# Turning by 64-row halves inside the half-array products of a transformer block

## The chip, the cores and the metric

The kernel runs on one core of one Trainium2 chip. The metric is the device time of one execution in microseconds: 720.22 us, the median of three runs (718.71 to 721.14). PE is TensorE, DVE is VectorE, ACT is ScalarE, POOL is GpSimd and SP is SyncE, which issues nearly all the DMAs.

## The reference

One PixArt block on x of shape (16, 256, 256): 16 batch entries, 256 tokens, width 256, 16 heads of 16, and a context of 256 tokens for each entry. Modulation vectors come from `silu(cond) @ W_mod`. Everything is float32.

```python
qkv = modulate(ln(x), shift_a, scale_a) @ W_qkv + b_qkv
x = x + gate_a * (attention(q, k, v) @ W_proj + b_proj)
q_c = ln(x) @ W_qc + b_qc
k_c, v_c = split(ln(context) @ W_kvc + b_kvc)
x = x + attention(q_c, k_c, v_c) @ W_cproj + b_cproj
h = gelu(modulate(ln(x), shift_m, scale_m) @ W_mlp1 + b_mlp1)
out = x + gate_m * (h @ W_mlp2 + b_mlp2)
```

## The kernel before

Each attention is a **unit**: 16 self-attentions (`s`) and 16 cross-attentions (`c`), 32 units n = 0 to 31 in the order s0 to s4, then s5, c0, s6, c1, ... s15, c10, and c11 to c15. A unit is computed in eight **beats** k = 0 to 7, written out by hand in `beat` (line 1103); every engine runs in program order (`InOrder`, line 39), so the order in which `beat` issues is the order on each queue. After the units comes the MLP, with whole 128-row products, which the change leaves alone.

A beat n, k holds work of several units. In `visit` (line 1079) PE first makes the scores of the *next* unit in one direction, four `s` products into the only tile `sp` (names `s<-big`), from which DVE takes the row maxima with one TENSOR_REDUCE (`s_tile`, line 697). Then come four `st` products, the scores of *this* unit the other way round with the negated maximum as an extra contraction row (row 63 of each half of `q`; `t_part`), which ACT exponentiates (`exp`, `pt<-st`). Both `sp` and `st` are single tiles: the next beat's `s` must wait for this beat's reduce, and the next `st` for this beat's exponential. In the even beats 16 `o` instructions follow (`av_part`, values times exponentials; four column strips of 32). In the odd beats 12 **slots** follow: projections of the units n+2 and n+3 and the output projection of unit n-2.

Those projections run in **lanes** (`lane`, line 451; `lanes`, line 471): a product over 128 rows is cut into two over 64, and PE's lower and upper 64 rows work on two different projections side by side, one instruction of each in a slot. A projection does its lower half in one odd beat and its upper half in the next one that has it: V and K in beat 7, Q and V in beat 1, P and Q in beat 3, K and P in beat 5. Values are float32r pairs: `xTh` and `xTl` are high and low parts. `s` and `st` also use 64-row halves (63 or 64 rows), but `o` uses all 128 rows.

Sources must be turned: a layer norm gives `xn` with tokens on partitions, and the projections want it the other way. `transposed.turn` (line 384) makes four 128x128 transpositions into one bank (`psT_s`, `psT_c`, `psT_q`), from which ACT makes `xTh`. Unit n+3's first source T[0] is turned in beats 0 and 2, two transpositions each, just after `o`. If unit n+3 is a cross-attention it has a second source T[1] (name `psT_q`), turned in beat 4. The maxima are turned as well: two per unit, one full 128-row transposition (`ident,mx`) each, in beat 0 (pairs 4 to 7 of this unit) and beat 4 (pairs 0 to 3 of the next). ACT negates them (`m`) and SP sends them into `q`. All of these are whole-array instructions that stand between `o` and the next beat's `s`.

Units n = 1 to 28 turn a T[0]; 16 of them, n = 3, 5, 7, ... 23 and 24 to 28, turn a T[1] too. Below, *with two* means a unit that turns two sources, and *with one* the 12 others.

PSUM has no room to spare: two banks for `st`, two for `sp`, one `gen` (V or P) and three `tr`, which T[0], Q, o, T[1], K, o take in turn.

Of the kernel before, what the change touches and what calls it, by code (L numbers as in the profile page):

```python
# [16 lines left out]
P = 128  # L17
# [4 lines left out]
def pixart_block(  # L22
# [53 lines left out]
    DVE.memset(wz, 0.0)  # L76
    ident = const.tile([P, P], F32, name="ident")
    make_identity(nc, ident)
    mhalf = const.tile([P, 2], F32, name="mhalf")
    POOL.memset(mhalf, -0.5)  # L80

# [295 lines left out]
    def transposed(src, name, scale=None, pool=False):  # L377

        o = Box()

        def place():
            o.ps = ps_gen(f"psT_{name}", SHORT)

        def turn(fs=range(KC)):
            if len(fs) == KC:
                place()
            for f in fs:
                for t in range(NT):
                    PE.transpose(o.ps[:, f * N + t * P:f * N + (t + 1) * P],
                                 src()[:, t, f * P:(f + 1) * P], ident)  # L390

        def high():
# [58 lines left out]
    def lane(o, half):  # L451
# [3 lines left out]
        for low in (False, True):  # L455
            for f in range(2):
                for k in range(KC):
                    for a, b in (((1, 0),) if low else ((0, 0), (0, 1))):
# [6 lines left out]
                        PE.matmul(o.ps[:, f * N:(f + 1) * N], *((x_, w_) if o.tok else (w_, x_)),  # L465
                                  start=o.fresh, stop=(half == 1 and low and k == KC - 1),
                                  skip_group_check=True)
                        o.fresh = False
                        yield

    def lanes(x, y):


        if x:
            x.ps, x.fresh = ps_gen(f"ps_{x.name}", LONG if x.tok else SHORT), True
        return zip_longest(*(lane(o, half) for half, o in enumerate((x, y)) if o))

    def run(steps, n=12):
        for _ in islice(steps, n):
# [2 lines left out]
    def to_stack(W, src, bias, dst, which, name):  # L482
# [19 lines left out]
        def high():  # L502
            o.hi = work.tile([P, KC, N], F32R, tag="qkh", name=f"h_{name}", bufs=3)
            for f in range(KC):
                ACT.activation(o.hi[:, f], o.ps[:, f * N:(f + 1) * N], AF.Identity, bias=bias[f])

        def low():
            if name == "k0":
                gap(work, 64, "gap_l")
            o.lo = work.tile([P, KC, N], F32R, tag="qkl", name=f"l_{name}", bufs=3)  # L510
            if name == "k0":
                gap(work, 192, "gap_mx")
# [66 lines left out]
    def build_pre(u):  # L579

        b = u.b
        u.mx = None
        if u.kind == "s":
            ln = layernorm(lambda: X[b], f"s{b}")
            u.ln = [ln]
# [111 lines left out]
    def s_tile(u, g, par, t, bank=None, home=sp):  # L697
# [8 lines left out]
        for j in range(2):  # L706
# [5 lines left out]
        if u.mx is None:  # L712
            u.mx = work.tile([P, 2, 2, 4, NT], F32, tag="mx", name=f"mx_{u.n}", bufs=3)
        mx = u.mx.rearrange("p f r a t -> p r f a t")
        a = slice(2 * (g % 2), 2 * (g % 2) + 2)
        if alone or apart:
            src = home[bank] if apart else sp[:, bank]
            DVE.tensor_reduce(mx[:, par, g // 2, a, t], src.rearrange("p (j n) -> p j n", j=2),
                              AX.X, ALU.max)
        elif bank == 1:  # L720
            DVE.tensor_reduce(mx[:, :, g // 2, a, t], home.rearrange("p r (j n) -> p r j n", j=2),
                              AX.X, ALU.max)
        yield

    def m_part(u, hf, pst=None):
        m_row(u, hf, m_turn(u, hf, pst))

    def m_turn(u, hf, pst=None):

        if pst is None:  # L730
            pst = ps_gen(f"psm_{u.n}_{hf}", SHORT)
        PE.transpose(pst[:16, :P], u.mx[:, hf].rearrange("p r a t -> p (r a t)"), ident)
        return pst

    def m_row(u, hf, pst):

        m = work.tile([16, P], F32R, tag="m", name=f"m_{u.n}_{hf}", bufs=1)
        ACT.mul(m, pst[:16, :P], -1.0)
        SP.dma_start(u.q[63:P:64, 4 * hf:4 * hf + 4, :].bitcast(F32), m.bitcast(F32))

    def t_part(u, pair, par):

# [22 lines left out]
    def in_turn(*pieces):  # L765

        for _ in range(2):
            for f in pieces:
                next(f)

    def av_part(u, g):

        if g % 2 == 0:
            u.po = ps_gen(f"o_{u.n}_{g}", SHORT).rearrange("p (g n) -> p g n", g=2)
        for c in range(NT):
            for h in range(4):
                par, pair = h // 2, 2 * g + h % 2
# [19 lines left out]
    for n, (kind, b) in enumerate(seq):  # L797
        u = Box()
        u.n, u.kind, u.b = n, kind, b
        u.v = vts[n % 3]  # L800
        u.q, u.k = qks[n % 3]
        u.pt = {}
        u.ready = False
        units.append(u)
    nu = len(units)

# [272 lines left out]
    def visit(n, k, home=sp, between=None):  # L1079
# [13 lines left out]
        in_turn(*t)  # L1093
        later.append(lambda: exp(units[n], k))

    def spare(n, gate=True):
        p1, _, p3 = (v and v.post for v in map(unit, (n - 1, n - 2, n - 3)))
        if p3 and not p3.added:
# [4 lines left out]
    def beat(n, k):  # L1103
# [25 lines left out]
        kp = None  # L1129
        if k == 5 and lx and n:  # L1130
            kp = lanes(q3.K, None if alone else p2)
        visit(n, k, between=kp and (lambda: run(kp, 2)))
        if k == 0:
            exps()
            if prev:
                av_part(prev, 3)
            if q3 and q3.ready:
                q3.T[0].place()
                pst = m_turn(cur, 1, q3.T[0].ps[:, N:])
                q3.T[0].turn((0,))  # L1140
            else:
                pst = m_turn(cur, 1)
            if prev:
                p1.pull_sums(1)
            m_row(cur, 1, pst)
            if q2:
                q2.K.low()
                q2.K.send_low()
# [3 lines left out]
                p2.low()  # L1152
        elif k == 1:
            exps()
            run(lanes(q2 and q2.Q, q2 and n and q2.V))
            if prev:
                p1.pull_values(1)
            if lc:
# [6 lines left out]
        elif k == 2:  # L1165
            exps()
            if cur:
                av_part(cur, 0)
            if q3:
# [8 lines left out]
        elif k == 3:  # L1178
            if q3:
                q3.T[0].high()  # L1180
            exps()
            if q3 and q3.kind == "c" and n < nu - 4:
                q3.T[0].full()
            if alone and p2:
                p2.proj(0)
                p2.proj(1)
# [1 line left out]
                run(lanes(p2, q2 and q2.Q))  # L1188
            else:
                run(lanes(q2.V, q2.Q))  # L1190
            if q3 and q3.kind == "s":
                q3.T[0].low()
            if prev and ls:
# [4 lines left out]
        elif k == 4:  # L1198
# [2 lines left out]
                p2.end()  # L1201
            if cur:
                av_part(cur, 1)
            if lx:
                lx.T[1].turn()
            if nxt:
                m_part(nxt, 0, st[:, 0] if lx else None)
            if q2:
                q2.Q.low()
                q2.Q.send_low()  # L1210
            if q3 and q3.kind == "c":
                if n < nu - 4:
                    q3.T[0].rest_pool()
                spare(n, not lc)
            if ls:
                ls.ln[0].steps[1]()
                ls.ln[0].steps[2]()
                ls.ready = True
        elif k == 5:
            exps()  # L1220
            run(kp or lanes(q3 and q3.K, (None if alone else p2) if n else q2.V))
            if cur:
                o_out(cur, 0)
            if lc:
                lc.ln[0].steps[1]()
                lc.ln[0].steps[2]()
                lc.ready = True
            if prev:
                p1.back()
            v = unit(n + 5)  # L1230
# [2 lines left out]
        elif k == 6:  # L1233
# [6 lines left out]
                cur.post.pull(0)  # L1240
            if q3 and p2:
                q3.vk = lanes(q3.V, q3.K)
                run(q3.vk, 1)
            if p3:
                p3.store()
            if lx:
                if lc:
# [3 lines left out]
        elif k == 7:  # L1251
            exps()
            if lx:
                lx.T[1].parts[2]()
            run(q3.vk if q3 and p2 else lanes(q3 and q3.V, q3 and q3.K))
            if late:
                p2.add()
                p2.added = True
# [114 lines left out]
```

## Time and profile before

| what | value |
|---|---|
| median of three runs | 720.22 us (718.71 to 721.14) |
| the profiled execution: span | 719.7 us |
| instructions in the profile | 22488 |
| mean granted TensorE clock | 0.999 |
| share of the span that DMA queue q1 took of 16 engines | 45.5% |

The profile page gives for each engine its busy time and share, the chain that ended last, and the costliest groups. The timeline lists instructions in order of time, neighbours that are alike merged into one row with a count: the first number is the start of the first in us from the start of the span, the second how long the row lasts until the end of its last one. A PE row ends only when its results are out, long after the next has started, so PE's pace is read from start to start. PEld rows are the weight loads that go ahead of the products.

### The profile page before, as it was taken

To read this page: it belongs to the slowest core of one execution; us is meant where nothing else is said; L and a number is where in the kernel's file an instruction comes from. 1 tells how busy PE (TensorE), PEld (TensorE's weight loads), DVE (VectorE), ACT (ScalarE), POOL (GpSimd) and SP (SyncE) were. 2 spreads that over 40 slices of the span, in tenths; PEclk is the share of its full clock that TensorE was granted. 3 is DMA by queue.
4 is the path that set the end of the run, shared out by engine and by line. 5 is a ranking of instruction groups with operands and counts; after the bars stand their busy time and mean duration, and the time that the engine had idled before them with its cause. 6 is when DMAs were issued, how large, how long until landed. Compare 5 with 4: busy or idle time off the path is not lost.

```text
span 719.7 us, 22488 instructions
## 1 busy us (share of the span) xinstructions
PE 710.4 (99%) x8993; PEld 592.3 (82%) x8993; DVE 567.8 (79%) x895; ACT 551.7 (77%) x955; POOL 520.6 (72%) x518
## 2 busy tenths in 40 slices
PE   9999999999999999999999999999999999999997
PEld 8777777777877778777787777777779999999997
DVE  5878888888888798888888888888675777777653
ACT  5677888888888788887888888887867677666661
POOL 7655778787776867776686798977857988656651
PEclk9999999999999999999999999999999999999999
DMA  7574455554545456454655656456323132313212
GB/s 236 183 233 157 160 170 178 175 179 160 167 151 196 162 176 191 163 166 153 195 167 176 210 174 195 156 192 196 95 78 103 59 87 61 88 46 88 66 39 74
DMA packets 81548, 106.15 MB, mean 147 GB/s; under 512 B 16610, under 2 KB 44548, under 8 KB 81444
## 3 DMA queue, kind: packets, MB, share of 16 engines
q1 hardware_dynamic: 80548, 104.37, 45.5%
q8 instruction: 71, 1.16, 0.7%
q10 hardware_dynamic: 896, 0.35, 0.2%
q14 instruction: 33, 0.27, 0.1%
HBM read 35.89 MB, written 8.98 MB: 62 GB/s over the span
## 4 chain that ended last, share of the span: by engine, by line
PE 94%; DVE 3%; POOL 2%; issue 0%; ACT 0%; POOLq 0%; ACTq 0%
PE s L51 18%; PE o L51 16%; PE st L51 16%; PE ph L51 12%; PE ps_qc L51 4%; PE ps_kc L51 4%; PE ps_k L51 4%; PE ps_q L51 3%; PE ps_v_c L51 3%; PE ps_v_s L51 3%; PE ps_P_s L51 2%; DVE mx L51 2%; PE ps_P_c L51 2%; PE psT_c L51 2%; PE psT_s L51 2%; PE psT_q L51 1%
## 5 line engine op out<-in xcount | busy, mean ns | idle before, releaser
L51 DVE TENSOR_REDUCE mx<-s 128x4 f32<-128x1024 f32 x252 | 307.9, 1222 | 73.5 <-PE s L51 70.1
L51 ACT ACTIVATE pt<-st 128x1024 f32<-128x1024 f32 x256 | 263.4, 1029 | 51.8 <-PE st L51 51.0
L51 PE MATMUL o<-pt,v 128*32 128x256 f32 x2048 | 137.1, 385 | 0.0
L51 PE MATMUL s<-big 63*128 63x256 f32 x1008 | 116.8, 305 | 1.7 <-DVE st_q L51 0.8
L51 PE MATMUL st<-big 64*128 64x256 f32 (+1 forms) x1040 | 107.7, 282 | 0.8 <-issue 0.4
L51 PE MATMUL ph<-xTh_m,wself 128*128 128x256 f32 x512 | 100.2, 281 | 0.0
L51 POOL TENSOR_TENSOR hl<-hf,hh 128x512 fp32r<-128x512 f32 x60 | 80.1, 1350 | 20.8 <-ACT hh L51 20.8
L51 PEld LDWEIGHTS s<-big 63*128 63x128 f32 x1008 | 77.3, 185 | 21.0 <-issue 7.1
L51 PEld LDWEIGHTS o<-pt,v 128*32 128x32 f32 x2048 | 53.4, 109 | 39.5 <-ACT oT L51 1.3
L51 PEld LDWEIGHTS st<-big 64*128 64x128 f32 (+1 forms) x1040 | 81.2, 186 | 3.6 <-ACT pt L51 1.5
L51 PEld LDWEIGHTS ph<-xTh_m,wself 128*128 128x128 f32 x512 | 82.3, 188 | 1.2 <-issue 0.4
L51 PE MATMUL ph<-xTl_m,wself 128*128 128x256 f32 x256 | 71.1, 278 | 0.0
L51 ACT ACTIVATE hf<-ph,bT 128x256 f32<-128x256 f32 x112 | 47.0, 473 | 22.1 <-PE ph L51 21.9
L51 ACT ACTIVATE hh<-ph,bT 128x256 fp32r<-128x256 f32 x112 | 47.0, 472 | 19.8 <-PE st L51 8.4
L51 PEld LDWEIGHTS ph<-xTl_m,wself 128*128 128x128 f32 x256 | 48.2, 188 | 0.0
L51 PE MATMUL s<-big,hh 128*128 128x256 f32 x256 | 45.6, 278 | 0.0
L51 DVE TENSOR_SCALAR xn_m<-x,mv_m,rs_m 128x256 f32<-128x256 f32 x28 | 33.5, 1237 | 14.8 <-POOL rs_m L51 14.8
L51 POOL TENSOR_SCALAR xn_q<-x,mv_q,rs_q 128x256 f32<-128x256 f32 x32 | 38.9, 1225 | 1.7
L51 POOL TENSOR_SCALAR xn_c<-c,mv_c,rs_c 128x256 f32<-128x256 f32 x32 | 38.9, 1226 | 1.7
L51 PE MATMUL st<-big,hh 128*128 128x256 f32 x224 | 40.0, 278 | 0.0
L51 PEld LDWEIGHTS s<-big,hh 128*128 128x128 f32 x256 | 38.8, 188 | 0.0
L51 POOL TENSOR_SCALAR rs_c<-mv_c 128x2 f32<-128x2 f32 x16 | 3.6, 228 | 48.3 <-DVE mv_c L51 48.2
(230 smaller groups left out, 2133.1 us busy)
## 6 DMA issues: line engine op xcount, KB each, us to landing
big<-h_k SPq DMA_DIRECT2D x32, 256.0 KB
big<-h_kc SPq DMA_DIRECT2D x32, 256.0 KB
big<-h_qc SPq DMA_DIRECT2D x32, 256.0 KB
big<-h_q SPq DMA_DIRECT2D x30, 256.0 KB
big<-l_k SPq DMA_DIRECT2D x16, 256.0 KB
g<-gd SPq DMA_DIRECT2D x16, 256.0 KB
U_s<-oT SPq DMA_DIRECT2D x32, 128.0 KB
R_s<-rd_s SPq DMA_DIRECT2D x16, 256.0 KB
```

Of the source, the lines that this page charges most:

```text
L51: i = f(*a, **k)
```

## The change

- `half(h)` turns a source by 64 rows: eight transpositions of 64x128 to 128x64 instead of four of 128x128. The lower four are made before `visit` in beat 1 (T[0]) and beat 5 (T[1]), the upper four inside the next beat's `visit`, between `s` and `st`. `turning` writes four of them and two instructions of the projection in the *other* half: t, product, t, t, product, t. The slots of beats 1 and 5 fall from 12 to 10; `uneven` runs what is left. Where there is no T[1], two plain slots are moved ahead of `visit` in beat 5.
- The maxima live in four fixed tiles `mxs` and are regrouped: pairs 2 to 5 of a unit are turned at the end of the unit before, pairs 6 and 7 together with pairs 0 and 1 of the next unit. Each group is turned by two halves (`m_half`) of 64 rows and 80 columns, in beats 2 and 3 and in beats 6 and 7, into the unused part of the bank of `o`.
- A product in the upper half waits for a copy by ACT that shows the lower half's bank is done (`behind`).
- The layer norm of a coming self-attention (aggregate on DVE, power and application on POOL) is issued in beat 5 instead of 4; the second copy of T[0] (`full`) goes ahead of the exponential of beat 3; `store` goes from beat 6 to 7.

```diff
+        def half(h):
+            rows = slice(64 * h, 64 * h + 64)
+            for f in range(KC):
+                for t in range(NT):
+                    c = f * N + t * P + 64 * h
+                    PE.transpose(o.ps[:, c:c + 64], src()[rows, t, f * P:(f + 1) * P], ident[rows, rows])
+                    yield
...
+    def turning(T, h, beside):
+        t = T.half(h)
+        for f in (t, beside, t, t, beside, t):
+            next(f)
...
+    def m_half(w, pst, h):
+        rows = slice(64 * h, 64 * h + 64)
+        PE.transpose(pst[:w.shape[1], rows], w[rows], ident[rows, rows])
...
+        if k == 1 and T0:
+            T0.place()
+            begin_of(q2.Q)
+            q2.V.behind = q2.K.copied
+            held["QV"] = side_by_side(q2.Q, q2.V)
+            turning(T0, 0, held["QV"][1])
+        if k == 5 and q3 and p2:
+            if T1:
+                T1.place()
+            begin_of(q3.K)
+            p2.behind = q2.Q.copied
+            held["KP"] = side_by_side(q3.K, p2)
+            if T1:
+                turning(T1, 0, held["KP"][1])
+            else:
+                uneven(held["KP"], 2, 2)
+        def between():
+            if k == 2 and T0:
+                turning(T0, 1, held["QV"][0])
+            if k == 6 and T1:
+                turning(T1, 1, held["KP"][0])
+            if k in (2, 6) and parts:
+                begin_o(cur, 0 if k == 2 else 2)
+                m_half(w, cur.po[:, 1, :P], 1)
+        visit(n, k, between=between)
...
-                pst = m_turn(cur, 1, q3.T[0].ps[:, N:])
-                q3.T[0].turn((0,))
...
-                q3.T[0].turn((1,) if q3.ready else (0, 1))
+            if q3 and not T0:
+                q3.T[0].turn()
...
+            m_half(w, cur.po[:, 1, :P], 0)
...
-            if lx:
-                lx.T[1].turn()
-            if nxt:
-                m_part(nxt, 0, st[:, 0] if lx else None)
```

What stands on PE around the start of beat 1, in the unit n = 17 (this unit turns `psT_c` and `psT_q`). Before, from the last `o` of beat 0:

```order
L51 MATMUL o_2_3831<-pt_7_3856,v_82 32x256
L51 MATMUL psT_c_3911<-ident,mx_3588 16x128
L51 MATMUL psT_c_3911<-ident,xn_c_3813 128x128 x2
L51 MATMUL s<-big_77 128x256 x4
L51 MATMUL st<-big_80 128x256 x4
L51 MATMUL ps_q_3939<-xTh_s_3703,wself 128x256
```

And now, at the same place:

```order
L51 MATMUL o_2_3895<-pt_7_3927,v_84 32x256
L51 MATMUL psT_c_3995<-ident,xn_c_3883 128x64
L51 MATMUL ps_v_s_3915<-wself,xTh_s_3773 128x256
L51 MATMUL psT_c_3995<-ident,xn_c_3883 128x64 x2
L51 MATMUL ps_v_s_3915<-wself,xTh_s_3773 128x256
L51 MATMUL psT_c_3995<-ident,xn_c_3883 128x64
L51 MATMUL s<-big_79 128x256 x4
```

The whole-array transpositions of the maxima and of half the source are gone from here; four half ones stand with two products of V. The second half comes in beat 2. Before, that beat ran `s`, `st` and `o`, and the transpositions followed its last `o`:

```order
L51 MATMUL o_0_3986<-pt_0_3900,v_83 32x256
L51 MATMUL o_0_3986<-pt_1_3937,v_83 32x256
L51 MATMUL psT_c_3911<-ident,xn_c_3813 128x128 x2
L51 MATMUL s<-big_77 128x256 x4
L51 MATMUL st<-big_80 128x256 x4
L51 MATMUL ps_P_s_4016<-wself,xTh_as_3924 128x256
```

Now they stand between `s` and `st`, with two products of Q and the upper half of a group of maxima, which goes into the bank of `o`:

```order
L51 MATMUL s<-big_79 128x256 x4
L51 MATMUL psT_c_3995<-ident,xn_c_3883 128x64
L51 MATMUL ps_q_3996<-xTl_s_3774,wself 128x256
L51 MATMUL psT_c_3995<-ident,xn_c_3883 128x64 x2
L51 MATMUL ps_q_3996<-xTl_s_3774,wself 128x256
L51 MATMUL psT_c_3995<-ident,xn_c_3883 128x64
L51 MATMUL o_0_4056<-ident,mxs 80x64
L51 MATMUL st<-big_82 128x256 x4
```

So after `o` nothing of the whole array is left before the next `s`, and `st` of beat 2 now stands behind a turning.

More of the change, by code (lines that the diff above doesn't have):

```diff
@@ L78, in pixart_block @@
     make_identity(nc, ident)
+    mxs = const.tile([P, 4, 80], F32, name="mxs")
+    POOL.memset(mxs, 0.0)
+    mxs = [mxs[:, i] for i in range(4)]
     mhalf = const.tile([P, 2], F32, name="mhalf")
@@ L511, in low @@
             if name == "k0":
-                gap(work, 192, "gap_mx")
+                gap(work, 192 + 128, "gap_mx")
             for f in range(KC):
@@ new lines, in m_part, with m_row @@
+    def m_part(u, hf):
+        pst = ps_gen(f"psm_{u.n}_{hf}", SHORT)[:16, :P]
+        PE.transpose(pst, mxs[2 + hf][:, :16], ident)
+        m_row(pst, (u, 4 * hf, 4))
+    def m_half(w, pst, h):
+        rows = slice(64 * h, 64 * h + 64)
+        PE.transpose(pst[:w.shape[1], rows], w[rows], ident[rows, rows])
+    def m_row(pst, *parts):
+        m = work.tile([16, P], F32R, tag="m", name="m", bufs=1)
+        ACT.mul(m[:pst.shape[0]], pst, -1.0)
+        row = 0
+        for u, pair, n in parts:
+            SP.dma_start(u.q[63:P:64, pair:pair + n, :].bitcast(F32), m[row:row + 4 * n].bitcast(F32))
+            row += 4 * n
@@ L1154, in beat @@
             exps()
-            run(lanes(q2 and q2.Q, q2 and n and q2.V))
+            if T0:
+                uneven(held["QV"], 10)
+            else:
+                run(lanes(q2 and q2.Q, q2 and n and q2.V))
             if prev:
@@ L1214, in beat @@
                 spare(n, not lc)
[L1215 to L1218, printed above, removed]
         elif k == 5:
             exps()
-            run(kp or lanes(q3 and q3.K, (None if alone else p2) if n else q2.V))
+            if q3 and p2:
+                uneven(held["KP"], 10 if T1 else 12)
+            else:
+                run(lanes(q3 and q3.K, (None if alone else p2) if n else q2.V))
             if cur:
                 o_out(cur, 0)
[L1224 to L1227, printed above, removed]
+            for l_ in (lc, ls):
+                if l_:
+                    l_.ln[0].steps[1]()
+                    l_.ln[0].steps[2]()
+                    l_.ready = True
             if prev:
@@ L1242, in beat @@
                 q3.vk = lanes(q3.V, q3.K)
-                run(q3.vk, 1)
-            if p3:
+                run(q3.vk, 0 if T1 else 1)
+            if p3 and not nxt:
                 p3.store()
```

94 lines of the change are left out of this document (56 added, 38 removed).

## The prediction

> **What bounds the kernel now.** I read the page first, then PE's timeline over one unit, then DVE's beside it.
>
> ```profile
> PE 710.4 (99%) x8993; PEld 592.3 (82%) x8993; DVE 567.8 (79%) x895; ACT 551.7 (77%) x955; POOL 520.6 (72%) x518
> ...
> PE 94%; DVE 3%; POOL 2%; issue 0%; ACT 0%; POOLq 0%; ACTq 0%
> ```
>
> PE is on 94% of the chain that ended last, so time taken off PE's queue should come off the total, as long as no other engine is just behind it. The windows of a unit with one source turned (n = 16) and one with two (n = 17), from one first `s` to the next, show who is:
>
> ```profile
> 283.54:298.83 15.29, 15.29 (x234) 11.96 (x231) 13.57 (x21) 12.70 (x21) 10.23 (x10) 1.00 0.60 190
> 298.83:314.74 15.91, 15.91 (x239) 12.45 (x237) 13.26 (x22) 13.38 (x22) 12.57 (x14) 1.00 0.45 152
> ```
>
> The columns are length, PE, weight loads, DVE, ACT, POOL, clock and DMA. PE has no gap; DVE is busy for 13.57 of 15.29 us. On averages that leaves 1.7 us a unit, but beats are less even. PE's timeline of beats 0, end of 2, 3 and 4 of n = 17:
>
> ```profile
> 298.83 0.50 PE L51 MATMUL s<-big 63*128 63x256 f32 x4
> 299.17 0.40 PE L51 MATMUL st<-big 64*128 64x256 f32 x4
> 299.50 1.07 PE L51 MATMUL o<-pt,v 128*32 128x256 f32 x16
> 300.50 0.28 PE L51 MATMUL psT_c<-ident,mx 128*16 128x128 f32 x1
> 300.62 0.38 PE L51 MATMUL psT_c<-ident,xn_c 128*128 128x128 f32 x2
> 300.93 0.51 PE L51 MATMUL s<-big 63*128 63x256 f32 x4
> ...
> 304.53 0.44 PE L51 MATMUL psT_c<-ident,xn_c 128*128 128x128 f32 x2
> 304.90 0.50 PE L51 MATMUL s<-big 63*128 63x256 f32 x4
> 305.24 0.41 PE L51 MATMUL st<-big 64*128 64x256 f32 x4
> 305.48 0.28 PE L51 MATMUL ps_P_s<-wself,xTh_as 64*128 64x256 f32 x1
> ...
> 306.85 0.42 PE L51 MATMUL s<-big 63*128 63x256 f32 x4
> 307.09 0.41 PE L51 MATMUL st<-big 64*128 64x256 f32 x4
> 307.43 1.07 PE L51 MATMUL o<-pt,v 128*32 128x256 f32 x16
> 308.43 0.66 PE L51 MATMUL psT_q<-ident,xn_q 128*128 128x128 f32 x4
> 308.95 0.28 PE L51 MATMUL st<-ident,mx 128*16 128x128 f32 x1
> 309.16 0.51 PE L51 MATMUL s<-big 63*128 63x256 f32 x4
> ```
>
> From start to start: four `s` take 0.24 after slots (306.85 to 307.09) and 0.34 after whole-array work (304.90 to 305.24), so coming back to row halves costs 0.10. Four `st` take 0.24 (305.24 to 305.48). Twelve slots take 1.37 (305.48 to 306.85), 0.114 each. `s`, `st` and `o` together take 1.60 (1.58 from 306.85, 1.67 from 298.83).
>
> **What is removed.** After `o`, the maxima and two transpositions of beat 0 take 0.43 (300.50 to 300.93), two of beat 2 take 0.37 (304.53 to 304.90), four and the maxima of beat 4 take 0.73 (308.43 to 309.16). In a unit with one source beat 4 has the maxima alone, 0.21:
>
> ```profile
> 293.06 0.28 PE L51 MATMUL psm<-ident,mx 128*16 128x128 f32 x1
> 293.27 0.50 PE L51 MATMUL s<-big 63*128 63x256 f32 x4
> ```
>
> So 1.53 us go from a unit with two and 1.01 from one with one. The return to row halves stays: something in halves still follows each `o`.
>
> **What a turning costs.** No row shows a transposition in half the rows beside a product, so I bound it. A whole one among 128-row products of the MLP:
>
> ```profile
> 548.60 0.28 PE L51 MATMUL s<-big,hl 128*128 128x256 f32 x1
> 548.72 0.60 PE L51 MATMUL psT_m<-ident,xn_m 128*128 128x128 f32 x4
> 549.08 0.36 PE L51 MATMUL ph<-xTh_m,wself 128*128 128x256 f32 x1
> ```
>
> The row of four lasts 0.60, a single one 0.28 (the maxima above): 0.32 for three steps, 0.11 each, and no pause between transposition and product. A transposition streams 128 columns; a half one streams 64, by proportion 0.055. Its weight load is still 128 columns wide, and loads show up in PEld (two answers for beat 4, one ending after the first load, one after the second; then lane products):
>
> ```profile
> 308.43 0.14 PEld L51 LDWEIGHTS psT_q<-ident,xn_q 128*128 128x128 f32 x1 [0.41 <-issue]
> 308.43 0.20 PEld L51 LDWEIGHTS psT_q<-ident,xn_q 128*128 128x128 f32 x2 [0.41 <-issue]
> ...
> 309.39 0.18 PEld L51 LDWEIGHTS ps_kc<-xTh_c,wkch 64*128 64x128 f32 x1
> 309.39 0.18 PEld L51 LDWEIGHTS ps_P_s<-wself,xTh_as 64*128 64x128 f32 x1
> 309.50 0.19 PEld L51 LDWEIGHTS ps_kc<-xTh_c,wkcl 64*128 64x128 f32 x1
> ```
>
> A second transposing load starts 0.06 after the first (0.20 less 0.14); loads of lane products follow at 0.11, the pace of the slots. I take 0.06, as the row of the same operation: four half transpositions in one half of the rows take 0.24, while the other half runs two products in 0.23. A turning is then 0.24. At least it costs 0.23, the two slots it replaces; at 0.11 a load it is 0.44. The Trainium skill speaks for the high end: "TensorE: Matmul & The Clock Gate", Part 2, section LDWEIGHTS, has a load take its columns over 1.2 per ns whatever its rows, 107 ns here, an estimate of 0.43 for a turning. The 0.06 step disagrees for transposing loads, the 0.11 of the lanes agrees; no run here shows one in half the rows. Half maxima: two pairs of halves a unit, 0.05 each (80 columns, 64 streamed), between nothing (beside the other half) and 0.12 (the whole one, 300.50 to 300.62).
>
> **The beats anew.** With two sources: beat 0 1.60 + 0.10 + 0.24 = 1.94; beat 1 0.24 + 0.24 + 10 slots = 1.62; beat 2 1.60 + 0.24 + 0.05 = 1.89; beat 3 0.34 + 0.05 + 0.24 + 1.37 = 2.00; beats 4 to 7 again 1.94, 1.62, 1.89, 2.00. Sum 14.90. With one: beat 4 1.60 + 0.10 + 0.23 = 1.93, beat 6 1.60 + 0.05 + 0.10 + 0.11 = 1.86, beat 7 0.24 + 0.05 + 0.24 + 1.25 = 1.78; sum 14.64. The same pieces in the old order give 2.03, 1.95, 1.97, 1.95, 2.33, 1.95, 1.81, 1.73 = 15.72 and, with beat 4 1.81, 15.20 (measured 15.91 and 15.29), so I compare ledger with ledger: PE alone would save 0.82 and 0.56.
>
> **What is late next.** Beats 1 and 5 get shorter than DVE's loop.
>
> ```profile
> 290.07 1.23 DVE L51 TENSOR_REDUCE mx<-s 128x4 f32<-128x1024 f32 x1 [0.56 <-PE s L51]
> 291.21 0.86 DVE L51 SCALAR_TENSOR_TENSOR xTl_s<-psT_s,sc,xTh_s 128x256 fp32r<-128x256 f32 x2
> 292.00 1.21 DVE L51 TENSOR_REDUCE mx<-s 128x4 f32<-128x1024 f32 x1
> 293.13 0.86 DVE L51 SCALAR_TENSOR_TENSOR l_qc<-ps_qc,bP,h_qc 128x256 fp32r<-128x256 f32 x2
> 293.91 1.21 DVE L51 TENSOR_REDUCE mx<-s 128x4 f32<-128x1024 f32 x1
> ...
> 307.31 1.23 DVE L51 TENSOR_REDUCE mx<-s 128x4 f32<-128x1024 f32 x1 [0.39 <-PE s L51]
> ```
>
> A reduce starts 0.46 after its `s` (306.85 to 307.31); the next `s` follows 1.27 after the reduce's start where it has waited (292.00 to 293.27); with a low part between, reduces are 1.92 apart. So `s` to `s` is at least 0.46 + 1.27 = 1.73, over the 1.62 of beats 1 and 5. The low parts of K (beat 0) and Q (beat 4) just fit: reduce 0 at 0.46, the next at 2.38 at the earliest, and `s` at 1.94 asks for it at 2.40. So beats 1 and 5 stand at 1.73, 0.11 more each. With one source T[0]'s low part follows reduce 3 and just fits as well: reduce 3 at 6.10 lets the next start at 8.02, and `s` of beat 4 at 7.56 asks for it at 8.02. Units become 15.12 and 14.86: 0.60 and 0.34 saved. Sum: 16 x 0.60 + 12 x 0.34 = 13.7 us.
>
> **The rest, at nothing.** The layer norm issued a beat later:
>
> ```profile
> 311.07 2.43 POOL L51 TENSOR_SCALAR xn_s<-x,mv_s,rs_s 128x256 f32<-128x256 f32 x2
> ```
>
> It ends at 313.50; a beat later that is 315.4, and its transposition now comes after `o` of the next beat 0, 314.74 + 1.60 = 316.3. If it is later still, PE waits with `s` and everything else queued. The new waits on ACT (`behind`) are for copies issued at the head of the same beat, 1.6 us before; were they late, the turning and `s` behind it would wait. The second copy of T[0], now ahead of the exponential of beat 3, delays it by one copy at most (0.58, the row of the same shape below), and twelve slots stand before the next `st` needs it. The upper maxima of beat 6 stand ahead of `st` and need the bank that ACT's copy of `o` frees; queued behind them are `st` and `o`, and the exponential waits for that `st`:
>
> ```profile
> 311.10 0.58 ACT L51 COPY oT<-o 128x512 f32<-128x512 f32 x1
> ```
>
> It ended 2.52 after the `s` of beat 5 (309.16). The maxima now come 1.73 + 0.48 = 2.21 after it, and `st` of beat 5, which sets ACT's start, about 0.33 sooner than in that beat (0.10 of return and 0.23 of slots that stood before it). So it just fits; half a copy late would be 0.3 x 16 = 5 us. SP gets 31 more small sends of maxima (95 for 64); those of beat 7 are needed in beat 2, over 3.5 us on. I take none of these, and no more than 5 us together.
>
> **The rivals.** First, PE's full gain, if DVE is looser than these rows: 16 x 0.82 + 12 x 0.56 = 19.8 us, 700. For it: beats 1 and 5 miss only by 0.11. Against: the 1.73 is made of rows without slack. Second, and slower: a half transposition loads at the pace of a lane product, 0.11, and a turning takes 0.44. The ledger with 0.44 gives 15.92 and 15.26, 0.20 and 0.06 more than the old one: 16 x 0.20 + 12 x 0.06 = 3.9 us slower, 724. Its place is the four (or two) turnings; each 0.1 us costs 16 x 0.4 + 12 x 0.2 = 8.8 us, so it decides from a turning of 0.24 + 13.7/88 = 0.40. The Trainium skill's rule for loads, above, comes out at the same 724. Third, the array empties between a transposition and a product of the other half, as it does around `o`: four changes of 0.10 and no overlap (0.24 + 0.23), 0.87 a turning, about 760. Against: the MLP rows change over without a pause, though there in the whole array. That the change does not do what it says can be excluded: the order shows the halves in place.
>
> **The numbers.** The sum is made against the profiled span, 719.7, which lies 0.5 under the median 720.22 and inside its 718.71 to 721.14; I take 13.7 off the median: 706. Its own range is 699 to 714 (half a copy of `o` or 0.06 a turning up, half the DVE term down). Chances: forecast 0.62; first rival 0.08; a turning between 0.30 and 0.38 (711 to 718) 0.07, of which 0.05 faster; second rival 0.14, of which 0.08 inside 722; third 0.06; others slower 0.03. What can be told from no change is 0.3%, 2.2 us. Faster: 0.62 + 0.08 + 0.05 = 0.75; same 0.10 (the rest of the third case and the second where it lands under 722); slower 0.15. The range 698 to 722 leaves out the slow cases and the ends, under 0.2.
>
> **What would show it.** Right: `psT` rows of 64 columns 0.06 apart beside slots at 0.11; units of about 15.1 to 15.3 and 14.9 to 15.0 us; `s` of beats 2 and 6 waiting for DVE by about 0.1; no wait at the upper maxima of beat 6. Wrong: half transpositions 0.11 or more apart, products of the other half standing still meanwhile, PE waiting for ACT's copy of `o` or POOL's `xn`, or units still at 15.3 and 15.9.

## The result and the profile after

The changed kernel takes 716.07 us (median of 5 runs, 714.10 to 717.74), the kernel before 719.89 us (5 runs, 718.71 to 721.14, on the same chip): a ratio of 0.9948 with a 95% interval of 0.9928 to 0.9967. It is faster by 3.8 us, where 13.7 us were forecast. The profiled execution spans 715.5 us in place of 719.7. The page of the kernel after, its engines and its chain:

```profile
PE 705.1 (99%) x9233; PEld 593.9 (83%) x9233; DVE 564.5 (79%) x895; ACT 551.0 (77%) x956; POOL 520.6 (73%) x519
...
PE 93%; DVE 3%; DMA 1%; issue 1%; POOL 1%; ACT 0%; SPq 0%; POOLq 0%; ACTq 0%
```

PE has 240 instructions more and is busy 5.3 us less; 1% of the chain is now DMA, which was not on it before. The windows of the same two units (n = 16 with one source, n = 17 with two) in the kernel after:

```profile
280.95:296.25 15.30, 15.30 (x241) 12.16 (x239) 13.57 (x21) 12.55 (x21) 10.34 (x10) 1.00 0.58 187
296.25:311.84 15.59, 15.59 (x250) 12.40 (x247) 13.18 (x22) 13.46 (x22) 12.44 (x13) 1.00 0.43 147
```

They were 15.29 and 15.91. By these, a unit with two sources gains 0.32 of the 0.60 that were forecast, one with one source nothing of its 0.34. The beats say where. This table has the median time from the first `s` of a beat to the first `s` of the next, over units 1 to 28, read from PE's timeline; the last rows belong to experiments below.

| kernel | sources | beat 0 | 1 | 2 | 3 | 4 | 5 | 6 | 7 | sum |
|---|---|---|---|---|---|---|---|---|---|---|
| before | two | 2.06 | 2.00 | 1.97 | 1.95 | 2.31 | 1.97 | 1.83 | 1.79 | 15.89 |
| forecast | two | 1.94 | 1.73 | 1.89 | 2.00 | 1.94 | 1.73 | 1.89 | 2.00 | 15.12 |
| after | two | 1.96 | 1.92 | 1.94 | 1.97 | 1.95 | 1.92 | 1.94 | 1.97 | 15.57 |
| before | one | 2.05 | 2.00 | 1.95 | 1.95 | 1.79 | 1.96 | 1.84 | 1.80 | 15.34 |
| forecast | one | 1.94 | 1.73 | 1.89 | 2.00 | 1.93 | 1.73 | 1.86 | 1.78 | 14.86 |
| after | one | 1.95 | 1.92 | 1.93 | 1.97 | 2.00 | 1.74 | 2.00 | 1.76 | 15.27 |
| e2, turning behind st | two | 1.84 | 2.04 | 1.92 | 1.98 | 1.83 | 2.05 | 1.95 | 1.96 | 15.57 |
| e3, other bank | two | 1.84 | 2.04 | 1.93 | 1.96 | 1.83 | 2.05 | 1.95 | 1.96 | 15.56 |
| e9, slot ahead | two | 1.91 | 1.85 | 2.02 | 1.97 | 1.90 | 1.85 | 2.07 | 1.96 | 15.53 |
| e15, no low parts | two | 1.96 | 1.81 | 2.03 | 2.00 | 1.95 | 1.80 | 2.05 | 2.00 | 15.60 |
| e5, short reductions | two | 1.95 | 1.69 | 1.92 | 1.98 | 1.95 | 1.69 | 2.16 | 2.00 | 15.34 |
| e5, short reductions | one | 1.94 | 1.69 | 1.93 | 2.00 | 1.99 | 1.63 | 1.90 | 1.80 | 14.88 |
| e6, before, short reductions | two | 2.00 | 1.95 | 1.95 | 1.95 | 2.31 | 1.96 | 1.83 | 1.80 | 15.76 |
| e6, before, short reductions | one | 2.02 | 1.95 | 1.94 | 1.95 | 1.79 | 1.95 | 1.83 | 1.75 | 15.17 |
| e7, and no half maxima | two | 1.87 | 1.69 | 1.87 | 1.97 | 1.89 | 1.69 | 1.87 | 1.97 | 14.81 |
| e7, and no half maxima | one | 1.88 | 1.70 | 1.90 | 1.95 | 1.92 | 1.63 | 1.86 | 1.85 | 14.69 |

All beats with two sources but 1 and 5 are within 0.05 of the forecast. Beats 1, and 5 with two, stand at 1.92 and not at 1.73; beat 5 with one does stand at 1.74, but beat 6 behind it at 2.00 and not at 1.86. PE's weight loads at the end of beat 0 and in beat 1 of n = 17 show the turning and what comes behind it:

```profile
297.92 0.13 PEld L51 LDWEIGHTS psT_c<-ident,xn_c 64*128 64x128 f32 x1 [0.41 <-issue]
297.93 0.18 PEld L51 LDWEIGHTS ps_v_s<-wself,xTh_s 64*128 64x128 f32 x1
297.98 0.14 PEld L51 LDWEIGHTS psT_c<-ident,xn_c 64*128 64x128 f32 x1
298.04 0.19 PEld L51 LDWEIGHTS ps_v_s<-wself,xTh_s 64*128 64x128 f32 x1
298.04 0.20 PEld L51 LDWEIGHTS psT_c<-ident,xn_c 64*128 64x128 f32 x2
...
298.39 0.31 PEld L51 LDWEIGHTS st<-big 64*128 64x128 f32 x4
298.86 0.18 PEld L51 LDWEIGHTS ps_q<-xTh_s,wself 64*128 64x128 f32 x1 [0.16 <-DVE l_k L51]
```

Half transpositions load 0.06 apart (297.92, 297.98, 298.04) while the other half's products go on at 0.11 (297.93, 298.04): the turning takes about 0.24. But the first product of Q waits for DVE's `l_k`. Q takes over the bank of K, and the low part of K is what reads that bank last. DVE in the same beats:

```profile
296.80 1.22 DVE L51 TENSOR_REDUCE mxs<-s 128x4 f32<-128x1024 f32 x1
297.94 0.87 DVE L51 SCALAR_TENSOR_TENSOR l_k<-ps_k,bqkv,h_k 128x256 fp32r<-128x256 f32 x2
298.73 1.22 DVE L51 TENSOR_REDUCE mxs<-s 128x4 f32<-128x1024 f32 x1
...
300.57 1.23 DVE L51 TENSOR_REDUCE mxs<-s 128x4 f32<-128x1024 f32 x1 [0.48 <-PE s L51]
```

The low part ends at 298.81 and Q starts at 298.86. So the first theory (A) was that this wait costs beats 1 and 5 their 0.19; its rival (B), that the turning itself, or coming back from it, does. The experiments found a third answer.

There are also single stalls. Units 1 to 28 took 440.28 us before and 438.76 after. By the medians, 16 x 0.32 + 12 x 0.07 = 6.0 us went; 4.5 us came back in a few units, most of all n = 23 (2.5 us over its kind) and 24 (1.3). PE's waits, SP's queue and windows of the kernel after at that place:

```profile
PE s L51 <- DMA big<-l_q: 2.2, 1, 2.2
```

```profile
397.30 1.20 SPq L51 DMA_DIRECT2D big<-m  x2
398.55 0.39 SPq L51 DMA_DIRECT2D cb<-cd  x1
398.98 0.43 SPq L51 DMA_DIRECT2D w<-in_L_xcond_W_mlp_dram  x1
399.45 1.23 SPq L51 DMA_DIRECT2D big<-h_q  x2
400.78 0.58 SPq L51 DMA_DIRECT2D big<-l_q  x1
```

```profile
403.00:407.30 4.30, 2.10 (x33) 1.91 (x34) 2.09 (x3) 2.55 (x6) 1.64 (x3) 1.00 0.94 238
407.30:411.50 4.20, 4.18 (x42) 2.77 (x44) 2.36 (x4) 1.61 (x2) 3.07 (x3) 0.59 0.69 234
```

The loads of the MLP's bias and first weight (`cb`, `w`) go out in front of Q's high and low parts. The DMA engines are 94% busy from 403.0 to 407.3, PE stands 2.2 us for `l_q` and then runs at a granted clock of 0.59. SP's queue at the same place in the kernel before:

```profile
399.24 0.32 SPq L51 DMA_DIRECT2D rd_c<-S_c  x1
399.62 0.42 SPq L51 DMA_DIRECT2D cb<-cd  x1
400.09 0.42 SPq L51 DMA_DIRECT2D w<-in_L_xcond_W_mlp_dram  x1
402.36 1.18 SPq L51 DMA_DIRECT2D big<-h_q  x2
```

There the loads went out 2.3 us and more ahead of Q's parts, 6.4 us into the unit; now it is 9.3 us. In between stand the two sends of maxima (`big<-m`) that the change puts at the end of beat 3: SP sends in order, and they go out at 397.30, when ACT's `m` is ready (397.27). Over the whole execution SP waits 58.9 us for `m`, where it waited 15.7.

### The profile page after: what moved, and what is told of

Same layout as the page of the kernel before. It is cut to its first block, busy times and chain, and to the rows that moved or that the text cites. A ratio compares the mean times of both kernels' runs of the same rounds, so it can differ in the third digit from the quotient of the medians.

```text
span 715.5 us, 23043 instructions
## 1 busy us (share of the span) xinstructions
PE 705.1 (99%) x9233; PEld 593.9 (83%) x9233; DVE 564.5 (79%) x895; ACT 551.0 (77%) x956; POOL 520.6 (73%) x519
## 4 chain that ended last, share of the span: by engine, by line
PE 93%; DVE 3%; DMA 1%; issue 1%; POOL 1%; ACT 0%; SPq 0%; POOLq 0%; ACTq 0%
PE s L51 18%; PE o L51 17%; PE st L51 16%; PE ph L51 12%; PE ps_qc L51 4%; PE ps_kc L51 4%; PE ps_q L51 4%; PE ps_k L51 3%; PE ps_P_s L51 3%; PE ps_v_s L51 2%; PE ps_v_c L51 2%; PE ps_P_c L51 2%; DVE mxs L51 2%; PE psT_m L51 1%; PE psT_s L51 1%; DMA big<-l_q 1%
## 5 line engine op out<-in xcount | busy, mean ns | idle before, releaser
L51 DVE TENSOR_REDUCE mxs<-s 128x4 f32<-128x1024 f32 x252 | 308.0, 1222 | 73.1 <-PE s L51 70.7
L51 PE MATMUL s<-big 63*128 63x256 f32 x1008 | 121.0, 302 | 3.6 <-DMA big<-l_q 2.2
L51 PE MATMUL st<-big 64*128 64x256 f32 (+1 forms) x1040 | 119.4, 288 | 0.4 <-ACT pt L51 0.4
L51 PEld LDWEIGHTS s<-big 63*128 63x128 f32 x1008 | 83.2, 186 | 31.4 <-DVE mxs L51 22.9
L51 PEld LDWEIGHTS st<-big 64*128 64x128 f32 (+1 forms) x1040 | 91.2, 186 | 3.0 <-ACT pt L51 1.5
L51 PE MATMUL ps_P_s<-wself,xTh_as 64*128 64x256 f32 x256 | 42.0, 294 | 0.0
L51 PE MATMUL ps_v_s<-wself,xTh_s 64*128 64x256 f32 x224 | 39.7, 299 | 0.0
```

Of the source, the lines that this page charges most:

```text
L51: i = f(*a, **k)
```

## The experiments

Ratios are to the kernel before, run on the same chip.

**e1, the bank freed by ACT.** `low()` of Q and K reads the high part instead of the bank:

```diff
-DVE.scalar_tensor_tensor(o.lo[:, f], o.ps[:, f * N:(f + 1) * N], bias[f], o.hi[:, f], ...
+DVE.scalar_tensor_tensor(o.lo[:, f], o.hi[:, f].bitcast(F32), bias[f], o.hi[:, f], ...
```

> The changed kernel, but in the units of the steady state the low parts of Q and K are worked out from the high parts in SBUF instead of from the PSUM bank (so the low parts of these are wrong, and the output with them); DVE still runs an instruction of the same shape at the same place. The bank that the next lane products need is then freed by ACT's copy alone. Theory A (the first slot of Q in beat 1, and of K in beat 5 with two sources, waits for DVE's low part, which frees its bank): beats 1, and 5 with two, fall from 1.92 to 1.73-1.76 us, 44 beats x 0.17 = 7.5 us: about 0.984 of the kernel before, 708 us (706 to 711). Rival B (the half transpositions, or the coming back to row halves, cost PE that time): beats 1 and 5 stay at 1.92, 716 us (0.995).

759.22 us, 1.0557 (1.0530 to 1.0584). A miss of both, because the instruction put in was not the same in cost. DVE and POOL in beats 0 and 1 of one unit of this run:

```profile
323.00 2.20 DVE L51 SCALAR_TENSOR_TENSOR l_k<-h_k,bqkv 128x256 fp32r<-128x256 f32 x2
```

```profile
322.88 0.61 POOL L51 CAST xTh_as<-U_s 128x512 fp32r<-128x512 f32 x1
323.57 1.35 POOL L51 TENSOR_TENSOR xTl_as<-U_s,xTh_as 128x512 fp32r<-128x512 f32 x1
```

With both operands in SBUF the low part takes 2.20 us in place of 0.87, and ends (325.20) when POOL's work does (324.92). The next reduction is late, and beat 1 takes 2.85 us. One thing can be read: Q's first product now comes 0.55 after `s` (median) in place of 0.67, so the wait for the bank is 0.12 long.

**e2, turning behind `st`.** The first half turning goes to where PE waits for the bank. The order of the two halves then has to be kept by something else than `s`: a one-column ACT copy of the turned half, for which the second half waits. The line that goes stood ahead of `visit`, the new one stands behind it and `exps`; T[1] alike in beat 5.

```diff
-            turning(T0, 0, held["QV"][1])
...
+                turning(T0, 0, held["QV"][1])
...
+        if h == 0:
+            T.seen = ACT.activation(dummy[:, :1], T.ps[:, 384:385], AF.Identity)
```

> The changed kernel, with the first half turning of each source moved from ahead of the s of beats 1 and 5 to behind their st (one tiny ACT copy per source is added, to order the two halves). Theory A: the turning fills part of the wait for the bank. s of beat 1 goes at 1.73 (DVE's loop), Q's first slot at 2.55 after the s of beat 0 (reduce 0.46 + 1.21, low part 0.86), ten slots and the return: 3.72 for beats 0 and 1 in place of 3.87; 44 x 0.15 = 6.6 us: 709.5 us (708 to 712), 0.986. Rival B: the turning costs the same wherever it stands: 716 us, 0.995.

714.79 us, 0.9939 (0.9921 to 0.9957). Beats 0 and 1 are 1.84 and 2.04, 3.88 together in place of 3.88: PE no longer waits for the bank, but now `s` of beat 1 waits for DVE's reduction.

**e3, another bank.** K is given its bank ahead of T[1] (with one source an empty tile takes T[1]'s turn), so Q takes over T[1]'s bank; the first half turning stands behind the fourth slot.

```diff
+            begin_of(q3.K)
             if T1:
                 T1.place()
-            begin_of(q3.K)
+            else:
+                ps_gen(f"none_{n}", SHORT)
...
+                uneven(held["QV"], 4, 4)
+                turning(T0, 0, held["QV"][1])
+                uneven(held["QV"], 6, 6)
```

> The changed kernel, with K given its bank ahead of T[1] (with one source, an empty place in the ring of three takes T[1]'s turn), so that Q takes over a bank that POOL or ACT freed long before and K one that was freed in beat 3 or 4; the first half turning moves behind the fourth slot of beats 1 and 5 (with the same tiny ACT copy). Theory A: no wait is left in beats 1 and 5; beats 0 and 1 together are held by DVE's loop alone, 0.46 + 1.92 + 1.27 = 3.65 in place of 3.87: 44 x 0.22 = 9.7 us, 706.5 us (705 to 710), 0.981. Rival B: 716 us, 0.995.

716.22 us, 0.9948 (0.9931 to 0.9965). The wait for `l_k` is gone from the waits of PE's weight loads, and beats 0 and 1 are 1.84 and 2.04 again; the loads of `s` now wait for DVE's reduction 102 times in place of 53. Theory A falls: the wait for the bank is there, but taking it away gives nothing back.

**e4, the loads behind Q.** The first entry of `W1P` goes from (-9, 3) to (-9, 4).

> The changed kernel, with the load of the MLP's bias and first weight issued one beat later (after beat 4 of unit 23 instead of after beat 3), so that they stand behind the sends of Q's high and low parts on SP. Theory A (PE's 2.2 us wait at the end of unit 23, and the slow clock behind it, come from l_q queued behind these loads): 716 - 3.7 = 712.5 us, 0.990. Rival (a delay of that one execution): 716 us, 0.995, and the wait at the same place or nowhere.

714.68 us, 0.9939 (0.9918 to 0.9960). Unit 23 takes its normal 15.55, but unit 24 takes 2.0 us over its kind: DVE stands for the context, whose load is now the one behind the weights, and with it the reduction of beat 2. DVE's waits for DMA in this run:

```profile
DVE st_c L51 <- DMA c<-in_ctx_dram: 1.7, 1, 1.7
```

**e5 and e6, DVE out of the way.** In both kernels the reductions of `s` take half of the columns.

```diff
-            DVE.tensor_reduce(..., home.rearrange("p r (j n) -> p r j n", j=2),
+            DVE.tensor_reduce(..., home.rearrange("p r (j n) -> p r j n", j=2)[:, :, :, :N // 2],
```

> The changed kernel with every reduction of s taken over half of its columns (the maxima are those of half of the keys, so the output isn't the reference's): DVE's loop falls from 1.73-1.82 to about 1.2 us, and the low parts end 0.6 us earlier, so that neither DVE nor the bank holds PE. What is left is PE's own work. Theory C (PE's pieces are larger than the prediction's ledger, and the waits of beats 1 and 5 are only a part): beats 1.95, 1.74, 1.94, 1.97 twice, units of 15.2 and 15.0 us; 716 - (16 x 0.37 + 12 x 0.29) = 706.6 us, 0.981 (0.978 to 0.985). Rival P (the ledger of PE was right, 14.90 and 14.64, and waiting for DVE took the rest): 716 - 18.4 = 697.6 us, 0.969.

> The kernel before with the same half reductions: what PE alone takes in the old order. Theory C: the old order waits for DVE little, units 15.7 and 15.2 in place of 15.89 and 15.34: 720 - 4.4 = 715.6 us, 0.994, so that PE alone gains about 9 us by the change. Rival P: the same here, but then PE alone gains 18 us.

After: 709.19 us, 0.9842 (0.9803 to 0.9881). Before: 714.69 us, 0.9925 (0.9900 to 0.9950). Between them are 5.5 us, where theory C had 9; units 23 and 24 of the changed kernel are 3.5 us over their kind in this run too. Two units of the changed kernel with short reductions (n = 16, 17):

```profile
278.62:293.50 14.88, 14.88 (x241) 12.00 (x239) 9.68 (x21) 12.50 (x21) 10.38 (x10) 1.00 0.57 189
293.50:308.87 15.37, 15.37 (x250) 12.36 (x248) 9.02 (x21) 13.47 (x22) 12.45 (x13) 1.00 0.47 159
```

DVE is busy for 9.0 and 9.7 us of a unit, and units still take 15.37 and 14.88. Beats 1 and 5 do fall to 1.69. Rival P (697.6) is out; theory C comes close (706.6), but beat 6 with two sources rises to 2.16. PE there, and ACT beside it:

```profile
305.11 0.28 PE L51 MATMUL psT_q<-ident,xn_q 64*128 64x64 f32 x2
305.39 0.25 PE L51 MATMUL o<-ident,mxs 64*80 64x64 f32 x1
305.39 0.54 PE L51 MATMUL st<-big 64*128 64x256 f32 x4
```

```profile
304.76 0.58 ACT L51 COPY oT<-o 128x512 f32<-128x512 f32 x1
```

The upper half of the maxima waits until ACT's copy of `o` (to 305.34) has freed the bank, and `st` behind it too: the wait that the prediction named and took at nothing. In the changed kernel itself it isn't there (1.94), because DVE holds PE back first. Without it, 0.24, PE's own unit is 15.10 with two sources.

**e7, no half maxima**, in the run with short reductions:

```diff
-                m_half(w, cur.po[:, 1, :P], 1)
...
-            m_half(w, cur.po[:, 1, :P], 0)
...
-        m_row(cur.po[rows_, 1, :P], *parts)
+        m_row(ident[rows_], *parts)
```

> The run with the changed kernel and half reductions, without the half transpositions of the maxima (ACT writes the row of maxima from a constant, so no maximum is subtracted before the exponential; all else stands). By the prediction's 0.05 for each, four to a unit: 30 x 0.20 = 6 us less than with them. Theory C (each puts the two row halves out of step, and the next whole-array work waits for the later half): 0.08 to 0.10 each, 10 to 12 us less. If they lie beside other work: no difference.

700.75 us, 0.9755 (0.9709 to 0.9802): 8.4 us less than with them. With one source the four halves cost 0.19 (forecast 0.20), with two 0.53, of which 0.24 is the wait in beat 6 and 0.29 their own. They show in beats 0 and 4 (1.95 to 1.87 and 1.89), one beat later than they run: the half that turned is behind the other, and `o`, which takes the whole array, waits for the later one.

**e8, the maxima alone.** `T0 = T1 = None`; the sources are turned whole, as before.

> The changed kernel with the sources turned whole at the places of the kernel before (two transpositions behind o in beats 0 and 2, four in beat 4), so that of the change only the maxima in halves and groups and the later layer norms are left. By the prediction's pieces: two whole maxima go (0.09 and, in beat 4, 0.18 or 0.11), four halves at 0.05 come: 0.07 less a unit, 718 us (0.997). Theory C with 0.09 a half: 0.09 more a unit, 722.5 us (1.003).

737.42 us, 1.0243 (1.0221 to 1.0266). With two sources the run is spoilt (K takes Q's bank right behind Q's low part, and beat 4 takes 2.96). With one source it can be read: 15.67 against 15.34 before, 0.33 more where theory C had 0.09 and the prediction's pieces 0.07 less. So with whole sources the half maxima are a loss. The run does not show how much of it is theirs alone: the later layer norms and, with one source, the two slots ahead of `s` in beat 5 are still there.

**e9, one slot ahead.** e3, with one slot of Q and V (or K and P) ahead of the `s` that waited:

```diff
+            uneven(held["QV"], 1, 1)
...
-                uneven(held["QV"], 4, 4)
+                uneven(held["QV"], 3, 3)
```

> The run with the other bank, with one slot of the lane pair moved ahead of the s of beat 1 (and of beat 5 with two sources), so that PE has work where it waited there for DVE's reduction, and comes to s already in row halves. Theory C (freeing the bank alone moved the wait to that s, 0.16, and made the s behind it a slow one): beat 0 is 1.67 + 0.22 = 1.89 and beat 1 0.24 + 0.24 + 0.24 + 9 x 0.114 + 0.09 = 1.84, 3.73 for the pair, and DVE allows 3.74 (reduce 1 at 2.46 with the low part between, 1.23, 0.05): 3.74 to 3.80 in place of 3.87, 44 x 0.10 = 4.4 us, 711.5 us (709 to 714), 0.988. Theory D (DVE's reduce, low part, reduce hold the pair at 3.86 in any order): 716 us, 0.995.

715.38 us, 0.9955 (0.9939 to 0.9972). The pair is 1.91 + 1.85 = 3.76, as theory C had it, and yet nothing is gained: beat 2 rises from 1.94 to 2.02. Its `s` has now waited for DVE.

**e10 and e11, whole maxima behind `o`**, one transposition each in beats 2 and 6, in the changed kernel and in e9.

> The changed kernel with the grouped maxima turned whole behind o of beats 2 and 6 in place of four halves. In the run with short reductions the four halves cost 0.31 with two sources and 0.19 with one; two whole ones cost 0.12 each by the row of before: 0.07 less with two, 0.05 more with one. Theory C: beats 0 and 4 fall by 0.07 (the halves come to o in step), beats 2 and 6 rise by 0.07: 716 us (714 to 717), 0.995. By the prediction's 0.05 a half: 0.04 more a unit, 717.2 us, 0.996.

> The run with the slot ahead and the whole maxima together: the sum of the two by theory C, 710.5 us (708 to 714), 0.987.

719.82 us, 1.0017 (1.0000 to 1.0033), and 721.48 us, 1.0046 (1.0032 to 1.0060): both misses. In e10 beats 0 and 4 fall by 0.06 to 0.10 as expected, but beats 2 and 6 rise by 0.13 to 0.20: the whole one starts 1.00 after the first `o`, where the next `s` starts in the changed kernel, and the next `s` comes 0.24 later, not 0.12.

**e12, e13 and e14, the loads early.** The first four entries of `W1P` go from beat 3 to beat 1, in e11, in the changed kernel and in e9.

> The run with both, and the MLP's bias and first four weight loads issued two beats earlier (after beat 1 of units 23 to 26, where the DMA engines are idle, instead of after beat 3, ahead of the sends of Q's high and low parts). Theory A (PE's wait for l_q at the end of unit 23, 2.2 us, and the half clock behind it, 1.3 us, are theirs): 3 us less than without, 707.5 us (705 to 711), 0.983, and no wait of over 0.7 us in units 23 and 24. Rival (another transfer is late in their place): no difference.

> The changed kernel, with nothing changed but the MLP's bias and first four weight loads, issued two beats earlier (after beat 1 of units 23 to 26). Theory A (the waits of units 23 and 24 are these loads' doing, in the changed kernel as well): about 2.7 us less than the changed kernel, as between the two runs with both: 713.4 us (712 to 715), 0.991, no wait over 0.7 us in units 23 and 24. Rival: 716 us, 0.995.

> The run with the slot ahead, with the same early loads: 715.4 - 2.7 = 712.7 us (711 to 715), 0.990.

718.83 us, 1.0005 (0.9992 to 1.0018); 713.36 us, 0.9903 (0.9880 to 0.9925); 712.67 us, 0.9895 (0.9873 to 0.9918). That is 2.65, 2.71 and 2.71 us less than the same kernel without; only the first pair ran on the same chip, and by the ratios the other two are 0.0045 and 0.0060 apart. (In the profiled e11 most of the stall, 1.7 us, stood in unit 26, where the last of the four loads goes out.) SP's queue in e13, unit 23:

```profile
394.07 0.59 SPq L51 DMA_DIRECT2D cb<-cd  x1
394.70 0.45 SPq L51 DMA_DIRECT2D w<-in_L_xcond_W_mlp_dram  x1
...
398.87 1.22 SPq L51 DMA_DIRECT2D big<-h_q  x2
400.19 0.54 SPq L51 DMA_DIRECT2D big<-l_q  x1
```

The loads go out 4 us ahead of Q's parts, in a pause of the queue and ahead of the maxima's sends, and no beat of units 23 and 24 stalls. e14 is the fastest version that ran, ahead of both kernels.

**e15, no low parts.** DVE's low parts of Q and K are left out; the reductions stay.

```diff
+            if name not in ("k0", "k1", "q0", "q1"):
+                o.lo = o.hi
+                return
```

> The changed kernel without the low parts of Q and K in the units of the steady state (the high part is sent in their place, so all three products use it; the sends stay): DVE has 0.87 us less in beats 0 and 4, and ACT's copy alone frees the bank. Theory C (the low parts hold beats 1 and 5, as they stand between two reductions and free the bank): beats 1, and 5 with two, fall from 1.92 to 1.73-1.77, units of 15.25 to 15.35 and 15.1 us: 716 - 6 = 710 us (708 to 712), 0.987. Rival D (the reductions alone, 1.83 from one waiting s to the next, hold the beats): 716 us, 0.995.

716.00 us, 0.9944 (0.9923 to 0.9965): rival D. DVE and PE in beats 1 and 2 of n = 17 of this run:

```profile
299.07 1.23 DVE L51 TENSOR_REDUCE mxs<-s 128x4 f32<-128x1024 f32 x1 [0.70 <-PE s L51]
300.21 0.24 DVE L51 BATCH_NORM_AGGREGATE mv_q<-st_q 128x2 f32<-128x6 f32 x2
300.89 1.23 DVE L51 TENSOR_REDUCE mxs<-s 128x4 f32<-128x1024 f32 x1 [0.45 <-PE s L51]
```

```profile
298.54 0.48 PE L51 MATMUL s<-big 63*128 63x256 f32 x4
...
300.35 0.51 PE L51 MATMUL s<-big 63*128 63x256 f32 x4
300.69 0.28 PE L51 MATMUL psT_c<-ident,xn_c 64*128 64x64 f32 x2
```

The same `s` of beat 2 and what follows it, in the changed kernel:

```profile
300.12 0.42 PE L51 MATMUL s<-big 63*128 63x256 f32 x4
300.38 0.28 PE L51 MATMUL psT_c<-ident,xn_c 64*128 64x64 f32 x2
```

DVE is idle for 0.70 ahead of the reduction, no low part is near and no bank is waited for. The reduction starts 0.53 after `s` (298.54 to 299.07), ends at 300.30, and the next `s` starts at 300.35: 1.81. And behind an `s` that has waited, the next work starts 0.34 later (300.35 to 300.69); behind one that came straight after slots, 0.26 (300.12 to 300.38; the median is 0.24). So the beat costs 1.81 and 0.10 more in the one behind it: 1.91, against 1.92 with the wait for the bank. Two limits of DVE, one through the bank and one through the reduction, stand at the same height, and whichever is lifted leaves the other.

## Why the prediction was wrong, and what was right in it

**Right.** PE bounds the kernel, and the change is faster, though 716.07 lies outside the sum's own 699 to 714. The turning by halves costs what was taken, 0.24, in spite of the weight loads: 0.06 apart beside products (the second rival, 724 us, had 0.11). The Trainium skill's rule ("TensorE: Matmul & The Clock Gate", Part 2, section LDWEIGHTS: a load takes its columns over 1.2, an estimate of 107 ns here) is not borne out by the 0.06 between the first and the second `psT_c` load above. The third rival, an array that empties between the halves (760), is out by the same rows. So is the first, PE's full gain (700), by beats 1 and 5. The layer norm a beat later costs one wait for `xn_s`, 0.6 us in unit 1, which e13 shows too (0.3) and e2, e3 and e4 don't; the `behind` waits cost nothing that PE's rows show.

**The step that failed** is "The beats anew" together with "What is late next". That DVE's loop becomes the bound in beats 1 and 5 was right, and was the mechanism; its size was not. "So `s` to `s` is at least 0.46 + 1.27 = 1.73" used a reduction that starts 0.46 after its `s`, as it does behind slots. Behind a turning it starts 0.53 after `s`, and an `s` that has waited gives 0.10 more to the beat behind it. 1.73 becomes 1.91, and beats 1, and 5 with two, came out at 1.92. With one source beat 5 is 1.74, as worked out, and the 0.10 is found in beat 6 (2.00 in place of 1.86). "The low parts of K (beat 0) and Q (beat 4) just fit" looked at the next reduction alone and not at the bank that the low part frees; that was a fault as well, but e3 and e15 show that it costs nothing beside the first.

**The sum, as the runs give it.** PE's own unit, from the run with short reductions, is 15.10 and 14.88 in place of 14.90 and 14.64. Part of it is named: beats 1, and 5 with two, are 1.69 where the ledger had 1.62, and with two sources the half maxima cost 0.29 where it had 0.20. Waiting for DVE is 15.57 - 15.10 = 0.47 and 15.27 - 14.88 = 0.39 in place of 0.22. That is 16 x 0.20 + 12 x 0.24 = 6.1 us of PE's pieces, and 16 x 0.25 + 12 x 0.17 = 6.0 us of waiting. On the other side the ledger of before was too low by 0.17 and 0.14, 4.4 us, most of which was DVE's hold too (15.89 falls to 15.76 and 15.34 to 15.17 with short reductions). 13.7 + 4.4 - 6.1 - 6.0 = 6.0 us, which is what the regular beats saved.

The two profiled executions are 4.2 us apart. Of these, 1.5 lie in units 1 to 28 (6.0 less 4.5 of stalls), 0.6 ahead of them and in units 29 and 30, and 2.1 behind the last `s`, which no term of the prediction forecast.

**At nothing** stood SP's 31 extra sends and what is queued there. Whether the maxima come in time for beat 2 was asked; what the sends do to the loads behind them was not. They wait for ACT, and the MLP's loads, which had gone out well ahead of Q's parts, now go out right in front of them. About 2.7 us of the stalls come from there; e12, e13 and e14, with the loads ahead of these sends, give them back three times.

**Open.** From the last `s` on, the trace is 2.1 us shorter (201.2 before, 199.1 after, and between 198.9 and 200.4 in all kernels built from the changed one, 201.3 in e6); all of it in the last 145 us, the MLP, which the change leaves alone. About 1.6 of it is PE's pace, without a wait: from 597.1 on, 60 products take 7.07 us before and the same 60 take 6.80 after, and more such stretches follow, at a granted clock of 1.00. e6, the kernel before with short reductions, has them at the same products; e9 has some at others. The other 0.6 lies behind the last product. Together they are half of the profiled gain. The cause was not found; as far as the prediction goes, this half is luck. With one source 0.17 of PE's 0.24 is not taken apart either.

## What to carry to other kernels

When work is taken off the leading engine, work out the loop of the engine behind it with the worst start that any beat will have, and count what a wait does to the work behind it: here 1.73 was 1.91. A wait seen in the trace is not yet its price: lift it (another bank, another order) and see whether the next limit stands at the same height. And a new send in a queue that runs in order holds up all that stands behind it while it waits: here loads that nobody had touched went out 3 us later in their unit, and cost 2.7.

## What the hardware showed that was not expected

- Transpositions in one row half of PE run beside products in the other at their own pace, 0.06 and 0.11 apart. But a half that gets extra work falls behind, and the next work of the whole array waits for it: 0.07 per half maximum in beats 0 and 4.
- After a gap of 2.2 us PE's granted clock was 0.59 over the next 4.2 us, and unit 24 took 1.3 us more. The length of the gap alone does not decide it: in e5 the clock was 0.67 over the 4.2 us behind a gap of 1.7 us, in e7 it stayed at 1.00 behind one of 2.4 us.
- A low part (two DVE instructions) with both inputs in SBUF took 2.20 us beside POOL's work, 0.87 with one input in PSUM. It is the two together: in e1, single instructions with both inputs in SBUF took 0.47 to 0.48 us where POOL did nothing meanwhile (40 of 120), as with one input in PSUM, and up to 1.6 where it worked. The Trainium skill says that GpSimd shares its SBUF interfaces with VectorE and contends with VectorE instructions that have two SBUF inputs ("GPSIMD Engine Reference", section Key points); this trace agrees.
